# A graph network block on one core: keys and values from twelve-bit parts in three float32r passes

## The chip, the cores and the metric

The kernel runs on one core of a Trainium2 chip. The metric is the time of one execution on the device in microseconds (us); a comparison takes the median of several runs. The core has five engines with a queue each: PE (TensorE: matrix products, and transposes as products with an identity), DVE (VectorE), ACT (ScalarE), POOL (GpSimd) and SP (SyncE, which here only issues DMAs). In the profile PE is the matmuls and PEld the weight loads that go with them.

## The reference, cut to what matters

```
N, D, BS, M, H, DH, L = 1024, 512, 16, 256, 8, 64, 4     # everything float32
h = gcn(batch_norm(relu(layernorm(x))))                   # 1024 x 512
for i in range(L):
    q = (ln(h) @ Wq[i]) as 16 batches of 64 rows, 8 heads of 64
    k = (cond @ Wk[i]);  v = (cond @ Wv[i])               # cond: 16 x 256 x 512
    h = h + softmax(q k' / 8) v @ Wo[i]
    val, gate = split(ln(h) @ geglu_w[i] + geglu_b[i])    # 512 -> 2 x 2048
    h = h + (val * gelu(gate)) @ ffo_w[i] + ffo_b[i]
out = x + gcn(h) + relu(layernorm(x))
```

cond is the same for all four layers, but Wk and Wv differ, so the keys and values (4096 x 512 by 512 x 512, twice) are new in each layer. The outputs have to agree with float32 arithmetic.

## The kernel before, in words

The 1024 rows of h are eight blocks of 128; block g is batches 2g and 2g+1, and is called group g. Per layer and group the kernel makes the transposed keys kT (512 features by 512 rows of cond) and the values v (512 rows by 512 features), the scores, the softmax, and the mix of the values; then come the output projection and, after group 7, the feed-forward part (FFN) in four rounds.

**Products by block sums.** A product of 512 x 512 by 512 x 512 is cut into 2 x 2 blocks and made from 7 block products in place of 8, with sums of the blocks beforehand and of the results afterwards. `seven` (L730) does it in one level: 28 matmuls of 128 x 256. `KeyPair` (L1235, with `InStep` L1015) makes the keys of two groups at once and takes four of the seven products apart once more: 52 matmuls of 128 x 256 for two groups. `QueryPair` (L1409) does the same for the queries of layers 1 to 3; layer 0 uses `QueryQuad` (L1371), one level. Block sums of weights and of cond are made on POOL (`weight_sums`, `sum_cond`, `cond_rights`, `inner_lefts`), results are added up on DVE. These matmuls are plain float32: the trace has two records for each, so that a product of four matmuls appears as "x8".

**float32r.** The FFN (`Chunk`, L1124) and the graph steps already use another way: a float32 operand is split into a high part of twelve bits, a rest, and their difference; the type float32r lets PE multiply such parts in one pass. `Chunk` multiplies high by high and rest by rest into one bank (`begin`, L1170), ACT scales that bank in place by 1 + TINY (L1179), and PE adds the third product (`end`, L1185). Splitting is one ACT operation (L1112), one DVE operation (L1113) and one POOL operation (L1116) per operand.

**The order of the work.** The kernel is written in program order; a planner (Tile) orders each engine's queue by program position and by when it reckons operands ready, gives tiles their buffers and sets the waits. `tc.keep_in_program_order` (called `pin`) puts an instruction behind the one written before it on its engine. `tc.issue_after` and `waiting_for` are narrower versions. In the attention, the matmuls of `KeyPair` and of its output projection are pinned; `seven`, `scores` and `mix` are not. The FFN chunks are pinned on PE, ACT, DVE and POOL.

**Per group** (loop at L1660): `scores` (32 small matmuls into four PSUM banks; DVE maximum L794, ACT exponential L799, DVE scaling L804), then `values` of the next group, then `mix` (16 transposes of the probabilities, 64 small matmuls). After each odd group `pair_sums` and `KeyPair` follow, with `attn_out_pair` (14 matmuls of 128 x 256) between its steps.

**The seam between layers.** During the last FFN round `load_projections` (L1509) fetches the next Wk, Wv, Wq, Wo and cond of group 0; POOL makes the sums; two calls of `ffn_out` (L1321) finish h; `ready_first` (L1485) normalises four blocks of it on DVE (L174); `turn_first` transposes them (L186); the keys of group 0 follow.

**Buffers.** SBUF: 36 slots of 128 x 1024 float32, 10 tiles of 128 x 512 ("t512"), 6 more ("acc"). PSUM: eight banks of 128 x 512.

## Time and profile before

| | |
|---|---|
| median of 3 runs | 2421.82 us (2421.81 to 2423.09) |
| the profiled execution | 2421.72 us, its span 2419.5 us |
| PE busy | 2385.1 us, 99% |
| PEld busy | 1874.2 us, 77% |
| DVE busy | 1665.3 us, 69% |
| POOL busy | 1050.1 us, 43% |
| ACT busy | 838.0 us, 35% |
| DMA | 163.57 MB, mean 68 GB/s |

The profile's time is 0.1 us from the median. "busy" is the time in which an engine had an instruction in work. The time of one matmul among others is read from the start of one group of matmuls to the start of the next, since matmuls overlap and their ends are modelled. In the timeline a row has start, length, engine, line, operation, output<-inputs, shape and count, and in brackets the idle time before it and who ended it.

### The profile page before, as it was taken

What the parts mean: (1) busy time and instruction counts of PE and PEld (TensorE: products, weight loads), DVE (VectorE), ACT (ScalarE), POOL (GpSimd) and SP (SyncE); (2) the same over time, 40 slices, a digit from 0 to 9 for tenths busy, and PEclk for the clock granted to TensorE, in tenths of its full rate; (3) what the DMA queues carried; (4) which work ended last, traced back from release to release, by engine and by line L of the source; (5) the groups of instructions that cost most, each with busy time, mean ns of one, the idle gap of its engine ahead of it and who ended that gap; (6) DMA issues with size and microseconds to landing.
All of it is one profiled execution on the core that took longest, in us unless ns stands there. A gap on an engine that the chain in (4) does not pass through costs nothing. (4 is left out here: it accounts for less than half of the span.)

```text
span 2419.5 us, 35192 instructions
## 1 busy us (share of the span) xinstructions
PE 2385.1 (99%) x13032; PEld 1874.2 (77%) x13032; DVE 1665.3 (69%) x3252; ACT 838.0 (35%) x1784; POOL 1050.1 (43%) x1127
## 2 busy tenths in 40 slices
PE   7999999999999999999999999999999999999999
PEld 5678887577787888577787888577787888667787
DVE  9665666787776557777786556777785556778764
ACT  7323334343213334343313324433323323434320
POOL 0334443665553223565553223555554322456531
PEclk9999999999999999999999999999999999999999
DMA  6322220111302221011221211011131031011140
GB/s 183 116 78 109 101 97 19 44 44 53 122 32 79 78 72 36 22 57 45 80 90 70 79 62 53 10 53 53 44 135 70 14 127 36 19 52 38 51 148 36
DMA packets 118066, 163.57 MB, mean 68 GB/s; under 512 B 9256, under 2 KB 66928, under 8 KB 117888
## 3 DMA queue, kind: packets, MB, share of 16 engines
q1 hardware_dynamic: 115792, 155.81, 19.5%
q0 software_dynamic: 1376, 4.30, 0.5%
q8 instruction: 108, 1.77, 0.3%
q10 hardware_dynamic: 720, 1.11, 0.1%
q14 instruction: 70, 0.57, 0.1%
HBM read 138.12 MB, written 23.07 MB: 67 GB/s over the span
## 5 line engine op out<-in xcount | busy, mean ns | idle before, releaser
L1179 ACT ACTIVATE g<-g 128x512 f32<-128x512 f32 x192 | 112.1, 584 | 280.8 <-PE g L1165 278.5
L1116 POOL TENSOR_TENSOR gsa<-gha,gla 128x512 fp32r<-128x512 f32 x96 | 126.1, 1336 | 103.5 <-DVE gla L1113 103.5
L1116 POOL TENSOR_TENSOR gsb<-ghb,glb 128x512 fp32r<-128x512 f32 x48 | 69.7, 1453 | 219.7 <-DVE glb L1113 219.7
L799 ACT ACTIVATE pr<-sc,nmax 128x256 f32<-128x256 f32 x256 | 118.4, 472 | 83.0 <-DVE nmax L794 82.5
L1165 PE MATMUL g<-gr,gsa 128*128 128x512 f32 x384 | 136.6, 437 | 0.0
L1334 PE MATMUL fa<-wff,fT 128*128 128x256 f32 x512 | 122.4, 381 | 6.7 <-DVE kept L1344 6.7
L1003 POOL TENSOR_TENSOR kr<-ct,ct 128x256 f32<-128x256 f32 x48 | 36.9, 770 | 211.7 <-DVE pr L804 207.1
L1192 ACT ACTIVATE g<-g,gcols 128x512 f32<-128x512 f32 x96 | 67.5, 703 | 164.5 <-DVE g L1200 161.3
L300 PE MATMUL pa_v<-wv,ct 128*128 128x256 f32 x512 | 123.9, 385 | 0.0
L1165 PE MATMUL g<-gr,gha 128*128 128x512 f32 x384 | 122.8, 401 | 0.0
L300 PE MATMUL pc_v<-wv,ct 128*128 128x256 f32 x512 | 121.0, 379 | 0.0
L300 PE MATMUL pd_v<-wvs,ct 128*128 128x256 f32 x512 | 120.9, 379 | 0.0
L1165 PE MATMUL g<-gl,gla 128*128 128x512 f32 x384 | 118.6, 390 | 0.0
L1334 PEld LDWEIGHTS fa<-wff,fT 128*128 128x128 f32 x512 | 96.5, 190 | 26.9 <-DVE kept L1344 9.9
L300 PEld LDWEIGHTS pa_v<-wv,ct 128*128 128x128 f32 x512 | 94.9, 190 | 22.5 <-issue 9.2
L794 DVE TENSOR_REDUCE nmax<-sc 128x2 f32<-128x512 f32 x128 | 83.6, 678 | 41.2 <-PE sc L787 41.2
L300 PEld LDWEIGHTS pd_v<-wvs,ct 128*128 128x128 f32 x512 | 97.3, 190 | 13.2
L300 PEld LDWEIGHTS pc_v<-wv,ct 128*128 128x128 f32 x512 | 97.0, 190 | 13.0
L1165 PEld LDWEIGHTS g<-gr,gsa 128*128 128x128 f32 x384 | 72.0, 188 | 33.4 <-issue 16.3
L897 POOL TENSOR_TENSOR ou<-ou 128x256 f32<-128x256 f32 x12 | 8.7, 727 | 190.4 <-DVE ou L896 127.4
L1230 DVE SCALAR_TENSOR_TENSOR fT<-g,gcols,g 128x512 f32<-128x512 f32 x48 | 35.9, 748 | 79.9 <-ACT g L1192 79.9
L1227 PE MATMUL g<-ln3T,gy 128*128 128x512 f32 x192 | 90.4, 592 | 0.0
(520 smaller groups left out, 6392.8 us busy)
## 6 DMA issues: line engine op xcount, KB each, us to landing
ct<-cond_dram SPq DMA_DIRECT2D x72, 512.0 KB, 5.6
wff<-in_L_gnn_ffo_w_dram SPq DMA_DIRECT2D x32, 512.0 KB, 4.6
cond_dram<-ct SPq DMA_DIRECT2D x24, 512.0 KB, 3.0
gxb<-in_L_gnn_geglu_w_dram SPq DMA_DIRECT2D x96, 128.0 KB, 2.3
gxa<-in_L_gnn_geglu_w_dram SPq DMA_DIRECT2D x96, 128.0 KB, 2.3
cond<-in_L_gnn_cond_dram SPq DMA_DIRECT2D x32, 256.0 KB, 4.2
ct<-cond_dram SPq DMA_DIRECT2D x24, 256.0 KB, 5.7
wk<-in_L_gnn_Wk_dram SPq DMA_DIRECT2D x8, 512.0 KB, 6.0
```

Of the source, the lines that this page charges most:

```text
L300: each(nc.tensor.matmul(at, left[:, k, l0:l1], right[:, k, r0:r1], start=start and n == 0 and k == 0, stop=n == len(cols_of) - 1 and k == ...
L794: nc.vector.tensor_reduce(nmax, ps3, AX.X, OP.max, negate=True)
L799: nc.scalar.activation(pr3[:, a, :], ps3[:, a, :], AF.Exp, bias=nmax[:, a:a + 1], accum_out=tot[:, a:a + 1])
L897: t.tensor_tensor(p7, p7, u2, OP.add)
L1003: t.tensor_tensor(to, of, less, OP.subtract)
L1116: pin(nc.gpsimd.tensor_tensor(s_at, h_at, l_at, OP.subtract))
L1165: pin(nc.tensor.matmul(to, self.part(i, which)[:, k, :], self.rights[i][which].bitcast(F32R)[:, k, :], start=start and k == 0, stop=stop a ...
L1179: pin(nc.scalar.mul(to, to, 1.0 + TINY))
L1192: pin(nc.scalar.activation(to, of, AF.Gelu, bias=gcols[:, cg:cg + 1]))
L1227: pin(nc.tensor.matmul(d, self.last[:, k, :], self.rights[2][:, k, :], start=False, stop=k == 1, skip_group_check=True))
L1230: pin(nc.vector.scalar_tensor_tensor(f0, a, bias, g0, OP.add, OP.mult))
L1334: each(nc.tensor.matmul(to[:, q * M:(q + 1) * M], left[i][k][:, (2 * s + q) * P:(2 * s + q + 1) * P], right[i][:, k, :], start=start and q ...
```

## The change

Each 128 x 512 block of a group's keys or values becomes one unit, `Twelve`: 4 + 4 float32r matmuls of 128 x 512 (high by high, rest by rest, over four blocks of the inner dimension) into one bank, an ACT pass over the bank, 4 more matmuls (difference by difference), and a copy out on ACT or DVE in turn. `steps_of` starts a unit before it ends the one before. Four units make a group's keys, four its values. Block 0 of k0, v0 and k1 of layer 0, made early beside the graph steps, is one plain float32 product.

cond (as `raw_x`, two slots and 512 KB x 2 in DRAM per group, in place of seven blocks) is split for each layer and group by `split_cond`; Wk and Wv are split by `right_parts`, in layers 1 to 3 at the seam, in layer 0 ahead of the aggregation. `seven`, `InStep`, `KeyPair`, `QueryPair`, `cond_rights`, `inner_lefts`, `sum_cond` go. Queries use `QueryQuad` in all layers. Scores, transposes, mixing and the units are pinned on PE, with parts of the units put between the parts of `mix` by hand. `ready_first` scales on ACT. In layer 0 the transposes of cond are pinned at the end of a group. Unchanged lines and most removed ones are left out:

```diff
+    def turn_cond(g, by=(0, 1), each=lambda ins: ins):
+        t = slots_of(2, f"ct_0_{g}")
+        for i, ctile in enumerate(raw_conds.pop(g)):
+            pt = four(transposed(ctile, f"cond_{g}_{i}", each))
+            for k in range(2):
+                to, of = t[k][:, :, i * P:(i + 1) * P], pt[:, 2 * k:2 * k + 2, :]
+                if by[k]:
+                    nc.vector.tensor_copy(to, of)
+                else:
+                    nc.scalar.copy(to, of)
+        raw_x[0, g] = t
...
+            raw_x[l, g] = slots_of(2, f"ct_{l}_{g}")
+            for k in range(2):
+                nc.sync.dma_start(raw_x[l, g][k].rearrange("p a b -> p (a b)"),
+                                  cond_dram[g][:, 1024 * k:1024 * (k + 1)])
...
+    def left_parts(x, name):
+        parts = [slots_of(2, f"{n}_{name}") for n in ("ah", "al", "as")]
+        for h, l, s, x in zip(*parts, x):
+            nc.scalar.mul(twelve_bits(h), x, INWARD * TINY)
+            nc.vector.scalar_tensor_tensor(twelve_bits(l), h, -1.0 / TINY, x, OP.mult, OP.add)
+            for k in range(2):
+                nc.gpsimd.tensor_tensor(twelve_bits(s)[:, k, :], h[:, k, :], l[:, k, :],
+                                        OP.subtract)
+        return parts
+    def right_parts(x, name, room=None):
+        parts = [slots_of(2, f"{n}_{name}") for n in ("bh", "bl", "bs")]
+        for i, (h, l, s, x) in enumerate(zip(*parts, x)):
+            nc.scalar.mul(twelve_bits(h), x, INWARD / TINY)
+            for k in range(2):
+                hk, lk, sk = (t[:, k, :] for t in (h, l, s))
+                nc.vector.scalar_tensor_tensor(twelve_bits(l)[:, k, :], x[:, k, :], 1.0 / TINY, hk,
+                                               OP.mult, OP.subtract)
+                if room:
+                    more = room(f"{name}_{i}_{k}")
+                    nc.scalar.mul(more, hk, TINY)
+                    nc.gpsimd.tensor_tensor(twelve_bits(s)[:, k, :], lk, more, OP.subtract)
+                else:
+                    nc.vector.scalar_tensor_tensor(twelve_bits(s)[:, k, :], hk, -TINY, lk,
+                                                   OP.mult, OP.add)
+        return parts
+    def split_cond(l, g):
+        if g < NG:
+            if l == 0:
+                save_cond(g)
+            conds[g] = left_parts(raw_x.pop((l, g)), f"c_{l}_{g}")
+    conds = {}
+    def plain(to, left, c, right):
+        for k in range(KC):
+            nc.tensor.matmul(to, left[k // 2][:, k % 2, c * P:(c + 1) * P],
+                             right[k // 2][:, k % 2, :], start=k == 0, stop=k == KC - 1)
+    class Twelve:
+        def __init__(self, name, left, c, right, to, by):
+            self.name, self.left, self.c, self.right = name, left, c, right
+            self.to, self.by = to, by
+        def multiply(self, which, start, stop):
+            left, right = self.left[which], self.right[which]
+            for k in range(KC):
+                pin(nc.tensor.matmul(self.bank,
+                                     twelve_bits(left[k // 2])[:, k % 2,
+                                                               self.c * P:(self.c + 1) * P],
+                                     twelve_bits(right[k // 2])[:, k % 2, :],
+                                     start=start and k == 0, stop=stop and k == KC - 1,
+                                     skip_group_check=True))
+        def begin(self):
+            self.bank = bank(self.name)
+            self.multiply(0, True, False)
+            self.multiply(1, False, True)
+            nc.scalar.mul(self.bank, self.bank, 1.0 + TINY)
+        def end(self):
+            self.multiply(2, False, True)
+            if self.by:
+                nc.vector.tensor_copy(self.to, self.bank)
+            else:
+                nc.scalar.copy(self.to, self.bank)
+    def steps_of(units):
+        before = None
+        for u in units:
+            u.begin()
+            if before:
+                before.end()
+            before = u
+            yield
+        before.end()
+    def keys(l, g, wk, begun=None):
+        kTs[g] = begun or slots_of(2, f"kT_{l}_{g}")
+        return steps_of([Twelve(f"k_{l}_{g}_{c}", wk, c, conds[g], kTs[g][c // 2][:, c % 2, :], c % 2)
+                         for c in range(1 if begun else 0, KC)])
+    def values(l, g, wv, begun=None):
+        vs[g] = begun or slots_of(2, f"v_{l}_{g}")
+        return steps_of([Twelve(f"v_{l}_{g}_{c}", conds[g], c, wv, vs[g][c // 2][:, c % 2, :], c % 2)
+                         for c in range(1 if begun else 0, 2 * MB)])
+    kTs, vs = {}, {}
...
+    def begin(n, left, right):
+        a = bank(f"begun_{n}")
+        plain(a, left, 0, right)
+        nc.scalar.copy(begun[n][0][:, 0, :], a)
...
-    def seven(name, product, c11, c12, c21, c22, s1=None, beside=lambda ins: None,
...
+                        pin(nc.tensor.matmul(
+                            banks[2 * c2 + j][b * NPG:(b + 1) * NPG, a * M:(a + 1) * M],
+                            qT[g // 4][c2][pj, a, c0 + b * NPG:c0 + (b + 1) * NPG],
+                            kT[c2][pj, a, b * M:(b + 1) * M], start=True, stop=True))
...
+        turned = []
+        for c2 in range(2):
             pTs = []
             for j in range(2):
                 u = 2 * c2 + j
-                pt = transposed(probs[u], f"pr_{l}_{g}_{u}")
+                pt = transposed(probs[u], f"pr_{l}_{g}_{u}", each)
                 pT = t512(f"pT_{l}_{g}_{u}")
                 if j:
                     nc.vector.tensor_copy(pT, pt)
                 else:
                     nc.scalar.copy(pT, pt)
                 pTs.append(pT)
-            if last is not None:
-                between()
-                weigh(*last)
-            last = (c2, pTs)
-        weigh(*last)
+            turned.append(pTs)
+            hooks[c2]()
+        weigh(0, turned[0])
+        hooks[2]()
+        weigh(1, turned[1])
...
-    class InStep:
...
-    class KeyPair(InStep):
...
-    def cond_rights(l, g):
...
-    class QueryPair(InStep):
...
+    def scaled_by_act(blocks, mv, root, name):
+        n = len(blocks)
+        less = small.tile([P, 4], F32, tag="less", name=f"less_{name}", bufs=1)[:, :n]
+        nc.vector.scalar_tensor_tensor(less, mv.rearrange("p (n c) -> p n c", c=2)[:, :, 0], -1.0,
+                                       root, OP.mult, OP.mult)
+        for i, nb in enumerate(blocks):
+            xns[nb] = t512(f"xn_{name}_{nb}")
+            nc.scalar.activation(xns[nb], h[nb], AF.Identity, bias=less[:, i:i + 1],
+                                 scale=root[:, i:i + 1])
     def ready_first(l, blocks):
-        xns.update(norm(blocks, f"ln2_{l}_{blocks[0]}"))
+        name = f"ln2_{l}_{blocks[0]}"
+        scaled_by_act(blocks, *moments([h[nb] for nb in blocks], name), name)
...
+    wk = right_parts(raw_wk, "wk_0")
+    split_cond(0, 0)
+    wv = right_parts(raw_wv, "wv_0")
...
+        raw = [load_w(Wk[l], f"wk_{l}")]
+        load_cond(l, 0)
+        raw.append(load_w(Wv[l], f"wv_{l}"))
+        raw.append(load_w(Wq[l], f"wq_{l}"))
+        raw.append(load_row(ffo_b, l * D, f"ffb_{l}"))
+        load_cond(l, 1)
+        return raw
...
+        lnS = ln_sums(l)
         if l:
+            flow = keys(l, 0, wk)
+            for _ in range(4):
+                next(flow)
+            then = values(l, 0, wv)
+            next(then)
+            next(flow, None)
+            ready_first(l, left_to_turn[2:])
+            sum_first(nc.gpsimd, 0)
+            sum_first(nc.gpsimd, 1)
+            for _ in range(3):
+                next(then)
             turn_first(l, left_to_turn)
             sum_first(nc.vector, 2)
+            sum_first(nc.vector, 3)
+            next(then, None)
         else:
+            scale_first(1, deviations(mv_first[1], "ln2_0_4"))
             turn_first(0, [0, 1, 2, 3])
+            for _ in keys(0, 0, wk, begun["k0"]):
+                pass
             turn_first(0, [4, 5, 6, 7])
+            for nb in range(2):
+                sum_first(nc.gpsimd, nb)
+            for nb in range(2, 4):
+                sum_first(nc.vector, nb)
+            for _ in values(0, 0, wv, begun["v0"]):
+                pass
             fetch_cond(2)
+        split_cond(l, 1)
+        qT = queries(l, wq)
+        wo = load_w(Wo[l], f"wo_{l}")
+        if l:
+            load_cond(l, 2)
+        else:
+            turn_cond(2)
...
         for g in range(NG - 1):
             if g == NG - 2:
                 take_ln3()
                 raw = load_geglu(l, 0)
             probs = scores(l, g, qT, kTs.pop(g))
+            if flow:
+                next(flow, None)
+            if g == NG - 2:
                 with waiting_for(scores.last, mybir.EngineType.Pool):
+                    left = geglu_weights(l, 0, *raw)
+            if not g:
+                with waiting_for(scores.last, mybir.EngineType.Pool):
+                    wo7 = wo_sums(wo)
             if g in (1, 2):
                 fetch_x(2 * l + g - 1)
+            flow = keys(l, g + 1, wk, begun.pop("k1") if l == 0 and g == 0 else None)
+            for _ in range(4):
+                next(flow, None)
+            then = values(l, g + 1, wv)
+            oTs.append(mix(l, g, probs, vs.pop(g), (lambda: next(flow, None), nothing,
+                                                    lambda: next(then))))
+            flow = then
             if g in (1, 2):
                 base_of(2 * l + g - 1)
+            if l == 0:
+                fetch_cond(g + 3)
+            if g % 2:
+                blocks = pair_sums(l, g - 1, oTs)
+                oTs.clear()
+            split_cond(l, g + 2)
+            if l:
+                load_cond(l, g + 3)
+            next(flow)
+            next(flow)
+            if g % 2:
+                pair = attn_out_pair(g - 1, *blocks, wo7, bank(f"oab_{l}_{g}"), bank(f"ocd_{l}_{g}"),
+                                     pin)
+                next(pair)
+                if g > 1:
+                    moments_into(mv_kept[:, 2 * (g - 3):2 * (g - 1)], [h[g - 3], h[g - 2]],
+                                 f"ln3_{l}_{g - 3}")
             if g == NG - 2:
+                for nb in range(4):
+                    ln3_turn(nb)
+            next(flow)
+            if g % 2:
+                for _ in pair:
+                    pass
+            if g == NG - 3:
+                scale_kept()
+                ln3_norm(g - 1, g)
+            if g == NG - 2:
+                for nb in range(4, 6):
+                    ln3_turn(nb)
                 for nb in (g - 2, g - 1):
                     ln3_sums(nc.gpsimd, nb)
+            if l == 0 and g + 3 < NG:
+                turn_cond(g + 3, each=pin)
         oT, = oTs
...
+            raw_wk, raw_wv, wq, ffb = load_projections(l + 1)
             ffn_out(l, R - 1, 0, fT, wff, kept)
+            wk = right_parts(raw_wk, f"wk_{l + 1}")
+            with waiting_for(Gated.last, mybir.EngineType.Pool):
+                wq = weight_sums(wq, f"wqs_{l + 1}")
             ready_first(l + 1, [0, 1, 4, 5])
+            split_cond(l + 1, 0)
             ffn_out(l, R - 1, 1, fT, wff, kept)
+            wv = right_parts(raw_wv, f"wv_{l + 1}", acc_tile)
             turn_first(l + 1, [0, 1, 4, 5])
             left_to_turn = [2, 3, 6, 7]
```

434 lines of the change are left out of this document (46 added, 388 removed).

## The prediction

> **What bounds the kernel now.** I began with the page: span, engines, clock.
>
> ```profile
> span 2419.5 us, 35192 instructions
> ...
> PE 2385.1 (99%) x13032; PEld 1874.2 (77%) x13032; DVE 1665.3 (69%) x3252; ACT 838.0 (35%) x1784; POOL 1050.1 (43%) x1127
> ...
> PEclk9999999999999999999999999999999999999999
> ```
>
> TensorE is busy 99% of the span at full clock. Whatever removes PE time shortens the kernel, and whatever makes PE wait lengthens it. The view of waits, PE alone, says how much waiting there is to remove:
>
> ```profile
> PE fa L1334 <- DVE kept L1344: 6.7, 8, 0.8
> PE fd L1334 <- DVE fs L1310: 4.4, 11, 0.4
> PE edges L393 <- DVE high L379: 3.9, 1, 3.9
> ```
>
> Its longest entries lie in the FFN and at the start; none is in the attention. So the sum has two parts: the PE time of the changed products, and waits that do not exist yet. Then came PE's timeline of one layer's attention (queries from 721.22, two groups from 743.70 to 808.30), where each stage follows the last without a gap:
>
> ```profile
> 721.22 0.59 PE L1031 MATMUL qa<-ln2T,wq 128*128 128x256 f32 x2
> ...
> 733.31 1.88 PE L300 MATMUL qa<-ln2T,wq 128*128 128x512 f32 x4
> 735.03 1.88 PE L300 MATMUL qb<-ln2T,wq 128*128 128x512 f32 x4
> ...
> 743.70 1.96 PE L787 MATMUL sc<-kT,qT 64*64 64x256 f32 x32
> 745.59 1.99 PE L300 MATMUL pa_v<-wv,ct 128*128 128x256 f32 x8
> 747.42 1.89 PE L300 MATMUL pb_v<-wvs,ct 128*128 128x256 f32 x8
> ...
> 757.78 1.91 PE L186 MATMUL tr_pr<-ident,pr 128*128 128x128 f32 x16
> 759.62 2.13 PE L822 MATMUL po<-pT,v 128*64 128x64 f32 x64
> ...
> 808.30 1.96 PE L787 MATMUL sc<-kT,qT 64*64 64x256 f32 x32
> ```
>
> Prices come from start to start. From 747.42 to 757.78 lie six products of 4 float32 matmuls of 128x256: 10.36/24 = 0.432 us each. Two matmuls of 128x512 (four records) take 735.03 - 733.31 = 1.72, so 0.86 each. The queries took 743.70 - 721.22 = 22.5 us. The float32r price stands in the FFN's timeline:
>
> ```profile
> 1107.12 0.63 PE L1165 MATMUL g<-gr,gha 128*128 128x512 f32 x2
> ...
> 1109.86 0.63 PE L1165 MATMUL g<-gr,gsb 128*128 128x512 f32 x2
> ```
>
> Twelve matmuls of 128x512 lie between these starts: 2.74/12 = 0.228 us each, weight loads included.
>
> **The change part by part.**
>
> *Keys and values on PE.* Before: 32 groups of values and 8 of keys in one level, 28 matmuls each, 1120; 12 pairs of keys of 52, 624; together 1744 x 0.432 = 753.4 us. After: 256 units, 3 of them plain (4 x 0.86 = 3.44 us each, 10.3), 253 of 12 float32r matmuls, 3036 x 0.228 = 692.2; together 702.5. PE gains 50.9 us. The form is that of the FFN (128x128 weights, 512 columns), so I take the row as it is. All of this lies on the path, since PE does.
>
> *Queries in one level.* In layers 1 to 3, 2 x 7 products of 2 matmuls of 128x512: 28 x 0.86 = 24.1 in place of 22.5, a loss of 1.6 x 3 = 4.8 us. Net gain 46.1.
>
> *Mixing cut in two.* After the scores the first product took 747.42 - 745.59 = 1.83 us in place of 1.73: a change from small tiles to full ones costs 0.1. A unit's first half between the two parts of the mix adds one such change per group: 32 x 0.1 = 3.2 us.
>
> *Work moved off PE's path.* These rows price the splitting and the units' passes:
>
> ```profile
> L1113 DVE SCALAR_TENSOR_TENSOR gla<-gha,gxa 128x1024 fp32r<-128x1024 f32 x48 | 76.8, 1600 | 15.9 <-ACT gha L1112 15.9
> ...
> L1113 DVE SCALAR_TENSOR_TENSOR glb<-ghb,gxb 128x512 fp32r<-128x512 f32 x48 | 33.0, 687 | 15.8 <-ACT ghb L1112 15.8
> ```
>
> ```profile
> L1179 ACT ACTIVATE g<-g 128x512 f32<-128x512 f32 x192 | 112.1, 584 | 280.8 <-PE g L1165 278.5
> L1116 POOL TENSOR_TENSOR gsa<-gha,gla 128x512 fp32r<-128x512 f32 x96 | 126.1, 1336 | 103.5 <-DVE gla L1113 103.5
> ```
>
> A group's cond costs DVE 2 x 1.6 = 3.2 us and POOL 4 x 1.34 = 5.3; its eight units cost ACT 8 x 0.58 + 4 x 0.58 = 7.0 us and DVE 4 copies, 2.8 at 0.69. A group lasts 28 to 34 us on PE (1.9 scores, 21.9 units, 4 transposes and mix, half of a 6 us projection pair). With the softmax, about 6 us on DVE and 5 on ACT, no engine beside PE is much over half full. I cost this at nothing; its cover is PE's units, and without cover it would be about 8 us a group.
>
> *The softmax against the pinned order.* Its length stands in the timeline of all engines:
>
> ```profile
> 826.23 1.96 PE L787 MATMUL sc<-kT,qT 64*64 64x256 f32 x32
> ...
> 831.70 0.47 ACT L799 ACTIVATE pr<-sc,nmax 128x256 f32<-128x256 f32 x1
> ...
> 832.49 0.62 DVE L804 TENSOR_SCALAR pr<-pr,inv 128x256 f32<-128x256 f32 x2
> ```
>
> The last probabilities are ready 833.1 - 826.2 = 6.9 us after the scores start. In the new order PE has then: scores 1.9, the last end of the values 4 x 0.228 = 0.9, four begins and three ends of keys 44 x 0.228 = 10.0. The transposes come at 12.8, so the softmax has 5.9 us to spare, against passes and copies in its way of 4 to 5 us at most. The other place is the first unit's end at 1.9 + 0.9 + 1.8 + 1.8 = 6.4: its ACT pass is ready at 4.7, but may stand behind exponentials that run to 832.2 - 826.2 = 6.0, then takes 0.58. That is between 0 and 0.3 us of waiting a group; I take 0.1, or 2.8 us over the 28 groups that follow another.
>
> *DMAs and pinned transposes.* A group's cond is two loads of 512 KB in place of three and a half, issued on SP a whole group ahead, and Wo is loaded behind the queries, some 40 us before its sums are multiplied; nothing. In layer 0 the transposes of the cond three groups on are now pinned at a group's end, and the scores queue behind them:
>
> ```profile
> cond<-in_L_gnn_cond_dram SPq DMA_DIRECT2D x32, 256.0 KB, 4.2
> ```
>
> Its four loads are written behind the mix, whose transposes free their tiles; from there to the pinned transposes PE has three unit steps, 36 x 0.228 = 8.2 us. Landing takes 4.2 and the issues a little more, so I cost it at nothing; without cover it is about 4 us at each of five groups.
>
> *The seam.* Here an added engine's work has no cover. The view by windows and the timeline, layer 0 to 1:
>
> ```profile
> 650.00:660.00 10.00, 10.00 (x42) 7.53 (x41) 9.63 (x15) 1.99 (x3) 6.99 (x11) 1.00 0.89 339
> 660.00:670.00 10.00, 9.59 (x45) 8.12 (x44) 9.62 (x12) 0.00 (x0) 9.76 (x11) 1.00 0.01 2
> 670.00:683.00 13.00, 13.00 (x69) 11.56 (x69) 12.66 (x35) 0.89 (x2) 3.57 (x3) 1.00 0.42 135
> ```
>
> ```profile
> 665.15 3.02 DVE L1340 TENSOR_TENSOR hall<-kept,hall 128x512 f32<-128x512 f32 x3
> ...
> 677.27 1.91 DVE L174 TENSOR_SCALAR xn_ln<-hall,mv_ln,y_ln 128x512 f32<-128x512 f32 x4
> 679.09 1.89 DVE L1340 TENSOR_TENSOR hall<-kept,hall 128x512 f32<-128x512 f32 x3
> ...
> 681.47 1.91 PE L186 MATMUL tr_ln<-ident,xn_ln 128*128 128x128 f32 x16
> 683.21 1.89 PE L300 MATMUL pa_k<-ct,wk 128*128 128x256 f32 x8
> ```
>
> Columns two to six are PE, PEld, DVE, ACT, POOL: DVE has 1.1 us free in these 33 (10 - 9.63, 10 - 9.62, 13 - 12.66). The change brings it Wk's rest (4 x 0.69) and difference (4 x 0.69) and cond's rest (3.2), 8.7 us before the first keys can end, and takes the scaling (1.91) away: 6.8 more, 5.7 of them without room. The planner gives earlier lines priority, so Wk's operations and cond's go ahead of the adds of the last FFN output, and keys start late. What can lie behind 683.2: DVE finished three adds (1.89) at 681 and three more by 682.8 that the keys do not need; Wk's difference is first used 3.6 us after the keys start. The bounds are 0 (all of it slides behind) and 8 us (5.7 with nothing deferred, and adds of two SBUF inputs at 1.0 us in place of 0.63 beside POOL, as 3.02 and 1.89 for three say, on six of them). I take 3.5, in the middle: 10.5 us for three seams. Wv comes after, with 10.9 us of keys as its cover. In layer 0 Wk, Wv and cond are split beside the aggregation; I cost that at nothing.
>
> A rule that speaks against the change: the Trainium skill, "SBUF — State Buffer", section "Who interferes with whom", has a DVE operation with two SBUF inputs and a reading GpSimd operation lock each other out. The trace agrees (3.02 against 1.89 for the same three adds); it is inside the 8 us bound. A second is in the rivals.
>
> *The sum.* 2421.7 (the profiled run, 0.1 from the median) - 46.1 + 3.2 + 2.8 + 10.5 = 2392.1 us.
>
> **The rivals.**
>
> *The seams are hidden as well* (deferred adds are enough cover): 2392 - 10.5 = 2381, or 2376 without any wait or switch. For it: only 4 to 6 us per seam are missing. Against: DVE's 97% there.
>
> *Gain mostly spent.* Seams at 8 us (24 in all), and 0.5 us for each of 28 groups (14) by cond's 1.6 us operations falling into the softmax: 2421.7 - 46.1 + 3.2 + 38 = 2417. For it: 36 slots are just enough (parts of Wk, Wv, cond and the next cond are 6 each), so a split may start late. Against: DVE is half idle within groups.
>
> *The clock falls at the seam.* A mechanism of PE's speed after idling:
>
> ```profile
> 9.85 0.35 PE L397 MATMUL pc<-ident,prow 72*128 72x72 f32 x1 [3.58 <-DMA prow<-in_L_gnn_bn_b_dram]
> ...
> 10.47 3.65 PE L186 MATMUL tr_cond<-ident,cond 128*128 128x128 f32 x16
> ...
> 18.21 1.91 PE L186 MATMUL tr_cond<-ident,cond 128*128 128x128 f32 x16
> ```
>
> Behind 3.58 us of idling, sixteen transposes took 3.65 us, the same sixteen later 1.91. If a seam's wait does this, it costs 1.7 more, 5.2 in all: 2397. The Trainium skill, "TensorE: Matmul & The Clock Gate", section "What's actually happening", says that an idle window of about 3.4 us halves the clock; by it only a seam at the upper bound would pay. The start of the trace agrees with it, though the page's clock row does not show it.
>
> *Slower: the ACT pass becomes the wait.* Each of 253 unit ends needs the ACT pass on its own bank. Its cover is the next begin, 8 x 0.228 = 1.8 us, for 0.58. If the planner's order puts the pass behind an ACT operation that waits for DVE or for a later matmul, pinned PE waits and cannot do other work. At 0.3 us per end it costs 76 us: 2468. It decides from (46.1 - 3.2 - 13.3)/253 = 0.12 us per end. For it: those queues are the planner's, and the FFN's, which run with half this cover without waits, are pinned. Against: ACT is a third busy. That float32r does not pay in this form would need 0.243 us per matmul in place of 0.228 (46.1/3036 more), which no row shows.
>
> **How the numbers follow.** Forecast (2386 to 2400, with the clock case): 0.53. Seams hidden (2374 to 2386): 0.20. Mostly spent (2400 to 2420): 0.12, of which 0.03 ends above 2417. Slower by the ACT pass or another pinned wait: 0.15. The range 2374 to 2420 leaves out that last case. Differences under 0.2% (5 us) cannot be told from none: faster 0.82, same 0.03, slower 0.15.
>
> **What would show it.** In the changed profile: 3036 records on the line of the units' matmuls, 0.228 us apart; two groups from scores to scores in about 62 us in place of 64.6; PE's waits for DVE or ACT at the first keys of layers 1 to 3, some 3 us each; 24 us for queries. The forecast fails if PE waits for the ACT pass at most ends, or if the groups' waits come near 1 us.

## The result and the profile after

The changed kernel takes 2479.68 us (median of four runs, 2478.29 to 2480.42) where the kernel before takes 2421.82: the ratio is 1.0237, with a 95% interval of 1.0219 to 1.0255. It is slower by 58 us; forecast were 2392.1 us and a gain of 30. The prediction is wrong in its sign. The page of the changed kernel, span, engines and the row of TensorE in 40 slices:

```profile
span 2478.6 us, 33729 instructions
...
PE 2384.1 (96%) x12532; PEld 1775.7 (72%) x12532; DVE 1586.5 (64%) x3053; ACT 998.1 (40%) x2023; POOL 949.6 (38%) x851
...
PE   8999999999989999999989999999989999999999
```

TensorE idles 94.5 us (2478.6 - 2384.1) where it idled 34.4, and the three slices with an 8 behind the first are the three seams between layers. That it is as busy as before (2385.1), with 46 us less to do by the prediction's count, says that some of its products also take longer. The view of waits, TensorE alone (total in us, times, longest):

```profile
PE tr_ln L187 <- ACT xn_ln L1318: 20.3, 3, 7.3
PE k L348 <- ACT k L359: 18.1, 22, 2.9
PE fa L1195 <- DVE kept L1205: 13.6, 11, 2.3
PE oab L282 <- DVE ou L912: 7.4, 12, 0.8
PE ocd L282 <- DVE hall L919: 7.3, 12, 0.6
```

None of these stood in the kernel before, except 6.7 of the third. The first and third are the seams, the last two are the output projection of a pair of groups, and the second is spread over the groups (9.2), the seams (5.9) and the start (2.9).

Where the time went is read from the starts of the scores, which are there before and after. A stretch of groups runs from the scores of group 0 to those of group 7 of a layer, a seam from there to the first scores of the next layer. TensorE's timeline before, layer 1's end and layer 2's start, and after, layer 1 from first to last and layer 2's start:

```profile
957.96 1.96 PE L787 MATMUL sc<-kT,qT 64*64 64x256 f32 x32
...
1303.90 1.96 PE L787 MATMUL sc<-kT,qT 64*64 64x256 f32 x32
```

```profile
757.27 1.96 PE L803 MATMUL sc<-kT,qT 64*64 64x256 f32 x32
...
984.09 1.96 PE L803 MATMUL sc<-kT,qT 64*64 64x256 f32 x32
...
1332.93 1.96 PE L803 MATMUL sc<-kT,qT 64*64 64x256 f32 x32
```

The column "forecast" applies the prediction's own prices to each stretch. Start: three products of 28 x 0.432 go, three plain and six float32r units come, -9.6. Groups: three pairs of keys and seven groups of values, 152.1, go; 56 units (55 in layer 0) less the last third of the last come, and 0.2 a group. Seam: again 36.3 go, eight units and that third come, queries +1.6, and the 3.5 taken for the seam.

| stretch, us | before | forecast | after | off by |
|---|---|---|---|---|
| start to the first scores | 174.8 | 165.2 | 174.5 | 9.3 |
| seven groups, layer 0 | 223.0 | 221.9 | 233.8 | 11.9 |
| seven groups, layers 1, 2, 3 | 214.3 each | 215.9 each | 226.8, 227.2, 226.8 | 33.1 |
| seams 0-1, 1-2, 2-3 | 346.0 each | 337.6 each | 348.9, 348.8, 349.8 | 34.7 |
| last group to the end | 341.1 | 342.0 | 342.0 | 0.0 |

The five add up to 89 us, and 2480.4 (the profiled execution) less 2392.1 is 88.3. So three places have to be explained: the groups (45), the seams (35) and the start (9).

### The profile page after: what moved, and what is told of

Read it like the earlier page. It is cut to its first block, busy times and chain, and to the rows that moved or that the text cites. A ratio compares the mean times of both kernels' runs of the same rounds, so it can differ in the third digit from the quotient of the medians.

```text
span 2478.6 us, 33729 instructions
## 1 busy us (share of the span) xinstructions
PE 2384.1 (96%) x12532; PEld 1775.7 (72%) x12532; DVE 1586.5 (64%) x3053; ACT 998.1 (40%) x2023; POOL 949.6 (38%) x851
## 5 line engine op out<-in xcount | busy, mean ns | idle before, releaser
L302 POOL TENSOR_TENSOR as_c<-ah_c,al_c 128x512 fp32r<-128x512 f32 x128 | 189.3, 1506 | 543.8 <-DVE al_c L300 490.3
L359 ACT ACTIVATE v<-v 128x512 f32<-128x512 f32 x127 | 73.9, 582 | 222.4 <-PE v L348 222.4
L348 PE MATMUL k<-as_c,bs_wk 128*128 128x512 f32 x504 | 141.8, 404 | 18.1 <-ACT k L359 18.1
L348 PE MATMUL v<-bh_wv,ah_c 128*128 128x512 f32 x508 | 145.6, 408 | 0.0
L348 PE MATMUL v<-bs_wv,as_c 128*128 128x512 f32 x508 | 139.8, 397 | 0.0
L348 PE MATMUL k<-ah_c,bh_wk 128*128 128x512 f32 x504 | 139.1, 399 | 0.0
L348 PE MATMUL k<-al_c,bl_wk 128*128 128x512 f32 x504 | 136.5, 393 | 0.0
L348 PE MATMUL v<-bl_wv,al_c 128*128 128x512 f32 x508 | 136.3, 390 | 0.0
L348 PEld LDWEIGHTS k<-as_c,bs_wk 128*128 128x128 f32 x504 | 90.2, 189 | 45.9 <-ACT k L359 13.3
L348 PEld LDWEIGHTS v<-bs_wv,as_c 128*128 128x128 f32 x508 | 92.9, 188 | 28.7 <-issue 9.2
```

Source lines behind the costliest of these rows:

```text
L302: nc.gpsimd.tensor_tensor(twelve_bits(s)[:, k, :], h[:, k, :], l[:, k, :], OP.subtract)
L348: pin(nc.tensor.matmul(self.bank, twelve_bits(left[k // 2])[:, k % 2, self.c * P:(self.c + 1) * P], twelve_bits(right[k // 2])[:, k % 2, : ...
L359: nc.scalar.mul(self.bank, self.bank, 1.0 + TINY)
```

## The experiments

All times stand beside runs of the kernel before on the same chip (medians of 2421.7 to 2422.4); 2479.7 is the changed kernel. The stretches of each run are read as in the table. Runs whose edit leaves a stretch alone still differ there: by 1.0 us at a seam, and by up to 1.6 at the start.

**Inside the groups.** The theory is that three small things add up: changes of kind between products (from float32r units to float32 products of other shapes, and back), waits of the pinned output projection, waits for ScalarE's pass. The rival is that one of them is all. First the mix, which the change cuts by two unit halves. TensorE's timeline of the changed kernel:

```profile
836.54 1.18 PE L348 MATMUL k<-as_c,bs_wk 128*128 128x512 f32 x4
837.55 1.04 PE L187 MATMUL tr_pr<-ident,pr 128*128 128x128 f32 x8
...
839.60 1.20 PE L348 MATMUL v<-bh_wv,ah_c 128*128 128x512 f32 x4
840.63 1.08 PE L348 MATMUL v<-bl_wv,al_c 128*128 128x512 f32 x4
```

Four matmuls of a unit take 4 x 0.228 = 0.91 us among their like, but 837.55 - 836.54 = 1.01 and 840.63 - 839.60 = 1.03 behind a float32 product, without idle time (the first half of the mix stands where the row is left out).

```
-            oTs.append(mix(l, g, probs, vs.pop(g), (lambda: next(flow, None), nothing,
-                                                    lambda: next(then))))
+            oTs.append(mix(l, g, probs, vs.pop(g), (nothing, nothing, nothing)))
+            next(flow, None)
+            next(then)
```

> The four transposes and the two halves of the mix stand together again; the last key unit's end and the first value unit's begin come behind them. If the groups lose time by changes between float32 and float32r products (0.11 us each: 1.01 to 1.03 us from start to start behind a change in place of 0.91), four changes less in each of 28 groups are 112 x 0.11 = 12.3 us: 2467 us. If they lose it by waits for ScalarE and VectorE alone, no difference: 2480. If the copies of the transposed probabilities become a wait (0.6 us a group), 2480 - 12 + 17 = 2485.

Measured: 2466.83 us, 1.0183 [1.0166, 1.0200] of before, 12.9 us less than the changed kernel; the groups give 2.7, 2.7, 3.2 and 2.8 us. Per group that is 0.4, or 0.1 for each of four changes. Each of them changes type and shape at once; the prediction's row behind the scores (1.83 for 1.73) is a change of shape alone at the same price, so no run says that the type is what costs. The timeline of this run:

```profile
833.15 1.91 PE L187 MATMUL tr_pr<-ident,pr 128*128 128x128 f32 x16
834.99 2.12 PE L838 MATMUL po<-pT,v 128*64 128x64 f32 x64
837.04 1.19 PE L348 MATMUL k<-as_c,bs_wk 128*128 128x512 f32 x4
838.07 1.08 PE L348 MATMUL v<-bh_wv,ah_c 128*128 128x512 f32 x4
```

Transposes and mix stand without a gap, so no wait took the place of the changes.

Second, the output projection. In the changed kernel, product 1 (oab) follows at once on product 5 in the same bank, and product 2 (ocd) on product 3; each waits for VectorE to read what went before. In the kernel before, which pins these products as well, a product of `KeyPair` stands between. TensorE's timeline before, and after:

```profile
862.40 1.03 PE L300 MATMUL kc<-wo_sums,os 128*128 128x256 f32 x4
863.26 1.89 PE L1259 MATMUL kd<-ct,wk 128*128 128x256 f32 x8
864.99 1.03 PE L300 MATMUL kc<-wo,oT 128*128 128x256 f32 x4
```

```profile
882.03 1.03 PE L282 MATMUL oab<-wo_sums,os 128*128 128x256 f32 x4
883.58 1.13 PE L282 MATMUL oab<-wo,oT 128*128 128x256 f32 x4 [0.52 <-DVE ou L912]
884.55 1.03 PE L282 MATMUL ocd<-wo_sums,oT 128*128 128x256 f32 x4
886.18 1.10 PE L282 MATMUL ocd<-wo,om 128*128 128x256 f32 x4 [0.61 <-DVE hall L919]
887.21 1.96 PE L803 MATMUL sc<-kT,qT 64*64 64x256 f32 x32
```

```
-        product(1, a, False)
-        nc.vector.tensor_tensor(h11, a, h11, OP.add)
         product(3, c, False)
         nc.vector.tensor_tensor(h21, c, h21, OP.add)
         t.tensor_tensor(h21, u2, h21, OP.add)
+        product(1, a, False)
+        nc.vector.tensor_tensor(h11, a, h11, OP.add)
```

> In the output projection of a pair, product 3 comes ahead of product 1, so that no product follows at once on the add that reads its bank. If the two waits of each pair (0.52 to 0.81 and 0.61 us, 12 pairs) lie on TensorE's path, 14.7 us go: 2465. If TensorE only waits later, at the scores behind the pair, nothing: 2480.

Measured: 2458.42 us, 1.0146 [1.0130, 1.0163], 21.3 us less; each layer's groups give 5.0 to 5.3. TensorE's timeline of the same pair in this run:

```profile
875.11 1.03 PE L282 MATMUL oab<-wo_sums,os 128*128 128x256 f32 x4
875.98 1.03 PE L282 MATMUL ocd<-wo_sums,oT 128*128 128x256 f32 x4
...
878.66 1.96 PE L803 MATMUL sc<-kT,qT 64*64 64x256 f32 x32
```

Both waits are gone, and the gain is larger than the idle time shown: from 882.03 to 887.21 the changed kernel takes 5.18 us, this one from 875.11 to 878.66 3.55, so 1.6 a pair where 0.52 + 0.61 = 1.1 was shown as idle. A wait costs more than its number (883.58 - 882.03 is 1.55, and a product takes 0.86: 0.69 for 0.52).

Third, the statistics of the finished pair. In groups 2 and 4 of each layer VectorE does them between the scores and the first maxima, so the exponentials end later, and the unit's pass on ScalarE comes behind them. All engines' timeline of the changed kernel:

```profile
823.29 0.69 DVE L154 BATCH_NORM_STATS2 st_ln<-hall 128x6 f32<-128x512 f32 x1 [0.84 <-POOL hall L924]
823.90 1.27 DVE L810 TENSOR_REDUCE nmax<-sc 128x2 f32<-128x512 f32 x2
...
829.26 1.19 PE L348 MATMUL k<-as_c,bs_wk 128*128 128x512 f32 x4 [0.61 <-ACT k L359]
```

This edit was run together with the two above:

```
+                    with tc.issue_after(scores.last.ins):
                         moments_into(mv_kept[:, 2 * (g - 3):2 * (g - 1)], ...)
```

> The three edits inside the groups together: the mix whole, products 3 and 1 swapped, and the statistics of the finished pair issued behind the scores' softmax. The first two gave 12.9 and 21.3 us by themselves; if they add up, 34 us; the statistics stand ahead of the first maxima in two groups of each layer and TensorE waits 0.35 to 0.64 us there, so 3 to 5 more if they are the cause: 2441 to 2446. If the waits only move to another place, 2450 or more.

Measured: 2442.37 us, 1.0084 [1.0067, 1.0101], 37.3 us less. Layers 1 to 3 give 9.5 to 9.6 us in their groups, of which the first two edits gave 7.7 to 8.5, so the statistics are worth 1 to 2 a layer. The waits for ScalarE's pass in groups 2 and 4 (0.49 to 0.64 us) are gone; those in group 0 (0.59 to 0.86) and group 6 (0.35) stay and have another cause, which no run took out. Of the 11 us by which a layer's groups missed the forecast, these three are 9.5. What is left, 1.4, fits those two waits and the other changes of kind at the scores and the pairs (0.1 each); it was not taken apart.

Was it the written order as such?

```
-                pin(nc.tensor.matmul(self.bank, ...))     # also scores, mix, pair, cond transposes
+                nc.tensor.matmul(self.bank, ...)
```

> The changed kernel without the written order of TensorE in scores, units, mix, pairs and cond transposes: the planner places them. If the written order is what makes TensorE wait for pairs' adds and ScalarE's passes, the planner fills those 1.7 us a pair and 0.6 us a group: 2450 to 2460. If the waits and the changes between float32 and float32r are in the planner's order too, no difference or a loss: 2478 or more.

Measured: 2451.83 us, 1.0119 [1.0104, 1.0135]: 28 us less, nearly all in the groups (6.1 to 6.7 us a layer). The planner by itself alternates the banks of the pair, as the swap does, so the order as written cost more than it brought; but the planner's order is 9 us slower than the mended one, and it does nothing for the seams (-0.4 to +0.5).

**The seam.** Theory: VectorE's work for the splits stands ahead of what TensorE waits for. Rivals: VectorE is slowed by GpSimd; TensorE's half clock behind the waits. The changed kernel's timeline of all engines, layer 0 to 1:

```profile
684.03 1.27 DVE L313 SCALAR_TENSOR_TENSOR bl_wk<-wk,bh_wk 128x512 fp32r<-128x512 f32 x2
...
689.00 0.66 DVE L1205 TENSOR_TENSOR kept<-fa,kept 128x512 f32<-128x512 f32 x1
...
689.71 3.52 PE L1195 MATMUL fa<-wff,fT 128*128 128x256 f32 x8 [2.32 <-DVE kept L1205]
...
695.47 3.40 POOL L302 TENSOR_TENSOR as_c<-ah_c,al_c 128x512 fp32r<-128x512 f32 x2 [1.30 <-DVE a_ln L142]
695.92 1.22 DVE L144 TENSOR_TENSOR b_ln<-a_ln,y_ln 128x4 f32<-128x4 f32 x1
...
702.47 3.67 PE L187 MATMUL tr_ln<-ident,xn_ln 128*128 128x128 f32 x16 [5.63 <-ACT xn_ln L1318]
```

First eight operations on Wk, of which the row shows two (684.0 to 688.8) go ahead of the add that the next FFN product waits for. Then the layer norm's chain of 128x4 operations runs beside GpSimd's differences of cond and takes up to 1.22 us at a step. Both waits are followed by half speed: the FFN product takes 3.52 us (1.89 is usual), the sixteen transposes 3.67 (1.91). In the view by windows (columns as in the prediction), the column behind the five engines is the granted clock:

```profile
690.00:700.00 10.00, 6.84 (x24) 5.32 (x23) 10.00 (x17) 0.00 (x0) 5.90 (x4) 0.83 0.00 0
700.00:710.00 10.00, 7.53 (x32) 6.72 (x32) 9.97 (x27) 6.08 (x10) 5.66 (x4) 0.66 0.00 0
```

Wk's split taken from VectorE:

```
-            wk = right_parts(raw_wk, f"wk_{l + 1}")
+            wk = right_parts(raw_wk, f"wk_{l + 1}", by_act=True)   # h, l, s: nc.scalar.mul(part, x, INWARD / TINY)
```

> Leaves out part of the computation: in layers 1 to 3 the rest and the difference of Wk are scaled copies written by ScalarE, not VectorE's subtractions; TensorE's work is the same. If the seam is set by the amount of VectorE's work, its eight operations (4.8 us from 684.0 to 688.8) go from each of three seams, and the 1.6 us that the first FFN product behind them loses to the half clock: 3 x 4.8 to 3 x 6.4, 2461 to 2466. If it is set by VectorE's slowing beside GpSimd (behind 691 us), which stays, most of the gain is given back: 2475 or more.

Measured: 2457.11 us, 1.0143 [1.0126, 1.0160]: 22.6 us less, 7.0, 6.9 and 7.9 at the three seams, somewhat more than was expected. That is more than the 4.8 us of VectorE's time, so its work there does stand on the path, and the waits left behind it do not give the gain back.

All parts taken from VectorE and GpSimd:

```
-            wv = right_parts(raw_wv, f"wv_{l + 1}", acc_tile)
+            wv = right_parts(raw_wv, f"wv_{l + 1}", by_act=True)
-            conds[g] = left_parts(raw_x.pop((l, g)), f"c_{l}_{g}")
+            conds[g] = left_parts(raw_x.pop((l, g)), f"c_{l}_{g}", by_act=bool(l) and not g)
```

> Leaves out part of the computation: as the run with Wk, and also the parts of Wv and of the first group's cond in layers 1 to 3 are scaled copies written by ScalarE, so that neither VectorE nor GpSimd splits anything at the seam. If VectorE's added work alone counts, Wk's 4.8 and cond's 2.4 us go, with the half clock's 2 to 5: 3 x 8 to 3 x 12, 2444 to 2456. If the slowing beside GpSimd counts as well (seven small operations at 0.7 to 1.25 us in place of 0.15 ahead of the first scaling, some 5 us), the whole 14 us of each seam: 2438. If the seam is set by something else, such as the loads, no less than 2470.

Measured: 2468.73 us, 1.0191 [1.0174, 1.0208]. No expectation held: it is faster than the changed kernel by 11, but slower than the run that took only Wk. Its timelines of TensorE and ScalarE show why:

```profile
705.97 2.07 PE L358 MATMUL k<-as_c,bs_wk 128*128 128x512 f32 x4 [8.72 <-ACT k L369]
```

```profile
695.48 1.04 ACT L317 ACTIVATE bh_wv<-wv 128x1024 fp32r<-128x1024 f32 x1
...
705.31 1.07 ACT L369 ACTIVATE k<-k 128x512 f32<-128x512 f32 x2
```

The unit's pass, ready when its two products were, stands in ScalarE's queue behind six copies of Wv and the layer norm's copies. This is the mechanism of the prediction's "slower" rival, in one place.

To tell VectorE's own work from its slowing beside GpSimd, the next run gives VectorE more of it and GpSimd none:

```
-            wv = right_parts(raw_wv, f"wv_{l + 1}", acc_tile)
+            wv = right_parts(raw_wv, f"wv_{l + 1}")
+            # as_c of the first cond of layers 1 to 3: nc.vector in place of nc.gpsimd
```

> At the seams of layers 1 to 3 GpSimd's differences of the first cond (4) and of Wv (4) are VectorE's: VectorE gets 4 x 0.6 + 4 x 0.6 = 4.8 us more of work, GpSimd none. If GpSimd's operations are what stretches VectorE's small ones (some twelve at 0.66 to 1.25 us in place of 0.15, 8 us), each seam is 3 us shorter: 2471. If the amount of VectorE's work sets the seam, each is 4.8 longer: 2494.

Measured: 2461.18 us, 1.0159 [1.0142, 1.0176]: 18.5 us less, 5.7, 5.7 and 6.6 at the seams, twice what was expected, although VectorE has 4.8 us more to do at each. The same chain on VectorE:

```profile
691.21 0.15 DVE L144 TENSOR_TENSOR b_ln<-a_ln,y_ln 128x4 f32<-128x4 f32 x1
```

0.15 us in place of 1.22 at the same step. So the slowing beside GpSimd is shown, and taking GpSimd's work away wins more than VectorE's 4.8 us of added work lose. If those lie on the path in full, the slowing is worth some 10 us a seam (5.7 + 4.8); that sum is an estimate, since the edit also takes four scalings of Wv's parts out of ScalarE's queue (`more` in the diff), and their share was not taken apart. The Trainium skill, "SBUF — State Buffer", section "Who interferes with whom", says that a VectorE operation with two SBUF inputs contends with a GpSimd operation that reads SBUF. These rows agree (1.22 us beside GpSimd, 0.15 without), and they show the price where it hurts most, on operations that are almost all waiting.

The half clock, by useless transposes where TensorE idled (the run also pins the FFN products and the transposes around them):

```
+        to = bank(f"warm_{name}")
+        for i in range(n):          # 20 and 50 at each seam, 24 and 24 in layer 0
+            k = i % 4
+            pin(nc.tensor.transpose(to[:, k * P:(k + 1) * P], ident, ident))
```

> TensorE transposes the identity where it idled: 20 transposes ahead of the FFN product that waited 2.32 us and 50 ahead of the layer norm's transposes (5.63 us) at each of three seams, 24 ahead of the begun keys (2.84) and 24 ahead of the first key unit's end (2.90) in layer 0. If the idling halves the clock, and the half clock lies on the path, the begun keys take 3.4 us in place of 6.7 and the key units behind 133.4 us 3.6 in place of 5.3, 5.0 in the stretch to the first scores; at each seam the transposes and the first key products give 2.4, the FFN products up to 1.8 more: 12 to 17 us in all, 2463 to 2468. If VectorE's backlog sets the end of each seam and the half clock only lies beside it, the start's gain alone: 2475. If the extra transposes only stand in the way: 2480 or more.

Measured: 2480.33 us, 1.0242 [1.0225, 1.0259]: no difference. The seams read +1.0, +1.0 and +0.1, the start -2.1. The same windows and a row of TensorE's timeline:

```profile
690.00:700.00 10.00, 8.50 (x65) 7.85 (x63) 10.00 (x20) 0.49 (x1) 5.47 (x4) 1.00 0.00 0
700.00:710.00 10.00, 6.30 (x32) 4.58 (x32) 9.96 (x27) 7.69 (x16) 6.75 (x6) 1.00 0.00 0
```

```profile
710.04 1.56 PE L355 MATMUL k<-as_c,bs_wk 128*128 128x512 f32 x4 [3.21 <-ACT k L366]
```

The clock is full there (1.00 where 0.83 and 0.66 stood), and nothing is won: this run is 2.1 us ahead from its start on, VectorE's and ScalarE's rows stand just 2.1 us earlier than in the changed kernel, and so does the unit's third product (710.04 for 712.14), which now waits 3.21 us for the pass in place of 1.85. So VectorE's backlog, with ScalarE's queue behind it, sets the seam, and the half clock lies in its shadow. The Trainium skill, "TensorE: Matmul & The Clock Gate", section "What's actually happening", has the clock halve behind an idle window of about 3.4 us. The halving is there in the granted clock, though behind a single wait of 2.32 us, and here the measurement decides; behind a wait of the same 2.32 us in the run without GpSimd's work the product took 1.99 us, so the length of the wait alone does not settle it.

At the start the half clock does count. The plain product of the begun keys, TensorE's timeline of the changed kernel and of the run with all parts on ScalarE, whose edit leaves layer 0 alone:

```profile
86.49 6.74 PE L335 MATMUL begun_k<-ct,wk 128*128 128x512 f32 x8 [2.84 <-DVE v_deg L137]
```

```profile
86.57 5.13 PE L345 MATMUL begun_k<-ct,wk 128*128 128x512 f32 x8 [2.76 <-DVE v_deg L137]
```

That run's first scores come 1.6 us earlier (172.9 for 174.5). In all four runs that change only layers 1 to 3 this product takes 5.1 to 5.4 us, its end comes 0.7 to 1.5 us earlier, and the first scores 0.6 to 1.6. In the run with the transposes it takes 3.60 us, as the product of values ahead of it does here. So the half clock here lies on the path: 1.6 us by these runs, and 3.1 (6.74 - 3.60) as an estimate if all of it went.

Then the order of the seam, with the same arithmetic on the same engines. Two orders change at once, VectorE's and that of TensorE's first key units:

```
             ready_first(l + 1, [0, 1, 4, 5])
-            split_cond(l + 1, 0)                     # and Wk's split ahead of it
             ffn_out(l, R - 1, 1, fT, wff, kept)
+            wk = first_parts(l + 1, raw_wk)          # Wk and cond: rests first, then differences
...
+        for u in units:                              # keys(l, 0), l > 0
+            u.bank = bank(u.name)
+            u.multiply(0, True, False)
+        for u in units:
+            u.multiply(1, False, True)
+            nc.scalar.mul(u.bank, u.bank, 1.0 + TINY)
```

> The same arithmetic in another order at the seams: the splits of Wk and of the first cond come behind the FFN's last adds and the layer norm's statistics in program order, rests ahead of differences, and the four key units of the first group run in phases (four times the high parts, then four times the rests, then the differences), so that TensorE needs only ScalarE's high parts for its first 3.6 us. If the loss is the order (Wk's 4.8 us ahead of the adds that TensorE waits for, and the half clock behind), each seam gives 5 to 9 us: 2453 to 2465. If it is the amount of VectorE's work, the waits come back at the rests: 2475 or more.

Measured: 2455.28 us, 1.0144 [1.0127, 1.0161]: 24.4 us less, 8.5, 7.3 and 8.4 at the seams. What stays is GpSimd and a queue. Its rows:

```profile
696.45 6.99 POOL L342 TENSOR_TENSOR as_c<-ah_c,al_c 128x512 fp32r<-128x512 f32 x2 [3.14 <-DVE al_c L336]
```

```profile
714.57 1.52 ACT L1353 ACTIVATE xn_ln<-hall,less_ln,y_ln 128x512 f32<-128x512 f32 x2 [5.96 <-DVE less_ln L1349]
```

```profile
716.62 1.20 PE L370 MATMUL v<-bs_wv,as_c 128*128 128x512 f32 x4 [3.30 <-ACT v L381]
```

GpSimd's operations are stretched as well, beside VectorE's subtractions (3.5 us each for 1.34), and ScalarE's scalings of the second half of the layer norm, which wait 5.96 us for VectorE, hold up the pass on a value unit behind them.

**The start, and all together.** In layer 0 the first unit's end waits 2.90 us, for a like reason: ScalarE's copies wait for VectorE, whose small operations take 1.2 us beside GpSimd's sums of Wq (timelines of TensorE, VectorE and GpSimd, changed kernel):

```profile
132.37 1.17 PE L348 MATMUL k<-as_c,bs_wk 128*128 128x512 f32 x4 [2.90 <-ACT k L359]
```

```profile
127.97 1.22 DVE L139 TENSOR_SCALAR y_ln<-v_ln 128x4 int32<-128x4 int32 x1
```

```profile
127.87 1.28 POOL L226 TENSOR_TENSOR wqs<-wqs,wq 128x512 f32<-128x512 f32 x1
```

The last version puts together the groups' three edits, the late split in phases, no GpSimd at the seams, and two more:

```
-            ready_first(l, left_to_turn[2:])
+            ready_first(l, left_to_turn[2:], False)  # scaled by VectorE, not ScalarE
...
+    scale_first(1, deviations(mv_first[1], "ln2_0_4"))
     with waiting_for(scale_first.last, mybir.EngineType.Pool):
         wq = load_w(Wq[0], "wq_0")                   # and, behind it, the sums of Wq
```

> A version meant to beat both kernels, with the same arithmetic: the three edits inside the groups (37 us together), the late split in phases (8 us a seam) and no GpSimd work at the seams (6 us a seam), the second half of the layer norm scaled by VectorE so that ScalarE's passes on the units do not queue behind it, and in layer 0 the sums of Wq behind the second half of the layer norm. If the two seam gains add up, 2480 - 37 - 42 = 2401; if they are the same microseconds, 2480 - 37 - 25 = 2418. If VectorE's work (now 4.8 us more) is the limit at the seam after all, 2430 or more.

Measured: 2407.87 us in five rounds, 0.9941 [0.9927, 0.9954] of before. It beats both kernels, the one before by 14.5 us. The groups give 8.7 to 9.8 us a layer, the seams 9.2, 9.4 and 10.5, the start 4.7. The seam gains add up only in part (8 and 6 would be 14): VectorE is full there again. Two of its windows (VectorE is column four):

```profile
680.00:690.00 10.00, 9.95 (x48) 8.19 (x48) 10.00 (x20) 4.67 (x11) 0.00 (x0) 1.00 0.01 2
690.00:700.00 10.00, 7.44 (x23) 4.75 (x22) 9.75 (x31) 4.47 (x8) 0.00 (x0) 0.84 0.00 0
```

Against the forecast column the profiled execution of this run is still 18 us long: 4.6 at the start, 7.8 in the groups, 5.6 at the seams. No run took these apart.

## Why the prediction was wrong

*What was right.* The price of the units (four matmuls in 0.91 us, 0.228 each), the queries (732.95 to 757.27, 24.3 us), the last stretch, and that the seam is VectorE's. Two groups from scores to scores take 65.3 us (821.91 to 887.21) in place of the 62 that were to show it. That the saving on TensorE can be had, at least in part, is shown by the mended version, which is 14.5 us faster than before where the sum promised 30; whether some of its edits would help the kernel before as well was not tried.

*"I cost this at nothing" (work moved off TensorE's path).* This step failed, in the sense that it counted how full each engine is over a group and not where its work stands in the queue. The pass is covered by a begin, but there are 22 waits for it of 18.1 us in all: 9.2 in the groups, 5.9 at the seams, 2.9 at the start.

*"The softmax against the pinned order."* The place was right, the size was not: 2.8 us were taken, and the waits are 9.2, all in groups 0, 2, 4 and 6, at 0.35 to 1.06 each. In groups 2 and 4 the statistics come ahead of the maxima, an operation that was left out of the chain; that is worth 1 to 2 us a layer. What makes groups 0 and 6 wait stays open.

*"Mixing cut in two."* Mis-sized: one change of kind at 0.1 us was counted; a group has gained at least four, and taking four out gives 0.4. Over 28 groups that is 11.3 us in the trace (12.9 by the medians) for 3.2.

*A term that is missing.* The prediction counted the products of a pair (6 us) but no wait in them. They were pinned before as well, with products of `KeyPair` between them; the change takes these away and writes the last five one behind the other, two of them straight behind a reader of their own bank. The waits cost 1.6 us a pair, 21.3 in all: the largest single item in the groups.

*"The seam."* Mis-sized beyond its upper bound: 0 to 8 us, 3.5 taken; against the sum without any seam wait (334.1) it is 14.7 to 15.7. The bound counted VectorE's operations at their usual length. Two things lie outside it: the chain of tiny operations stretched up to eightfold beside GpSimd, which the prediction had weighed only on the wide adds, and ScalarE's queue, in which passes stand behind scalings that wait for VectorE.

*Layer 0's start, costed at nothing:* 9.3 us. The same two mechanisms are worth 4.7, which came back in the mended version; the half clock behind a wait of 2.84 us, which the mended version still has, is worth 1.6 more where it was shorter, and 3.1 in all as an estimate. The rest was not taken apart.

*The rivals.* "Gain mostly spent" had the right places and too small prices, and no case added the terms that failed together. "The clock falls" came true as an event; at the seams it costs nothing by itself, as the run with the transposes shows, and at the start, which the rival did not name, at least 1.6 us. The case "slower by the ACT pass or another pinned wait" had 0.15 and covers what happened, but only the pass was given a mechanism and a price; the pair's waits were not looked for. "The ACT pass becomes the wait" is true in part: 18.1/253 = 0.07 us per end, under the 0.12 from which it was to decide, so it did not decide alone. Of the two signs that the forecast fails, PE waiting at most ends did not come (22 of 253), and waits near 1 us a group did: 0.88 are shown, 14.7 in the pairs, 9.2 for the pass and 0.8 elsewhere over 28 groups.

## What to carry to other kernels

When a change hands work to engines that look half idle, cost it by the queue and not by the share: name, for each new operation that the bottleneck waits for, what stands ahead of it in its engine's queue and what that waits for in turn. An order written out by hand needs a distance between two products that share a bank with a reader in between, and what stood between them may be what the change takes away; alternating the banks was worth 21 us here. Where a chain of tiny VectorE operations lies on the path, keep GpSimd's two-input operations away from it, even at the cost of more VectorE work.

## What the runs showed that was not expected

- VectorE's 128x4 operations take 0.15 us alone and up to 1.22 beside GpSimd's subtractions; those take 1.34 us elsewhere and 3.5 in the run with the late split. Giving VectorE 4.8 us more work and GpSimd none (and ScalarE four scalings less) made a seam 5.7 us shorter.
- Waits of TensorE shown as 0.52 and 0.61 us cost 0.7 and 0.8 from start to start; without the two, shown as 1.1, a pair is 1.6 shorter.
- A change of kind between products (type and shape together) costs TensorE 0.1 us without any idle time shown, and it is counted as busy.
- A single wait of 2.32 us was followed by half clock in one run and not in another. At the seams, filling such waits with transposes brought nothing, since another wait took their place; at the start, where the product at half clock lies on the path, it cost at least 1.6 us.
